# Slots of the preparation in the shared scans: statistics three slots earlier, one more slot between engines, projected halves loaded four slots apart

## The chip, the core and the metric

The kernel runs on one core of a Trainium2 chip. The metric is the device time of one execution in microseconds, taken as the median of several runs. Below, PE is TensorE's matmul stream and PEld its weight loads, DVE is VectorE, ACT is ScalarE, POOL is GpSimd, and SP is the queue of SyncE, which here issues most of the DMAs. A line number such as L571 is a line of the kernel before.

## The reference

The input x has 32 sequences of 256 tokens with 256 channels. A recurrent block comes first, then two layers of windowed attention with a gated feed-forward, all in float32:

```python
xr, gate = split(x @ W_in.T, 2);  xr = xr + t_emb[:, None]      # 512 channels each
xc = silu(causal depthwise conv of 4 taps over time (xr) + b_conv)
xn = layernorm(xc) * ln_g + ln_b
Bm, Cm, dt = split(xn @ W_xproj.T, 3)                           # 16 states each
Ad = 1 + tanh(dt @ W_dt.T + b_dt) * 0.01 * A
Bd = Bm * minimum(norm(xn), 1.0)
h  = clip(h * Ad + outer(Bd, xn), -10, 10);  y_t = C_t . h      # one step per token
cond = ((y + D * xn) * silu(gate)) @ W_out.T
for l in range(2):  # attention: 8 heads of 64, rotary, window 128; FFN: 682 gated, GELU
    c = c + attention(shift(c)) @ wo;   c = c + ffn(shift(c))
out = x + c
```

The step over tokens is serial: 256 steps per sequence, each on the whole state.

## The kernel before

**Groups and chunks.** The 32 sequences are four groups of eight (`GB`). One scan serves a whole group: 16 states by 8 sequences fill the 128 partitions, and the 512 channels lie along the row, so a step is one instruction on VectorE, `step` (L716), on a tile of 128x512. The 256 tokens are cut into eight chunks of 32 steps (`CH`), so there are 32 chunks in all; a chunk's 256 rows (8 sequences by 32 tokens) are handled in two halves of 128 (`NJ`).

**Who runs beside whom.** Group 0's scan runs by itself (`alone` in the code). The scans of groups 1 to 3 share the chip with attention and feed-forward of the group before. The last group's attention runs when all scans are over. `scan_slots` merges the agendas of all scans into one list of slots, one slot for each step, and the main loop emits some slots after each of the eight stages that a sequence takes in a layer.

**The agenda.** `at(s, f, ...)` puts the call of f at slot s; `s0 = c * CH` is the slot of a chunk's first step, and its preparation has negative offsets, inside the steps of the chunk before. Two agendas are filled: the first mostly with work of VectorE, ScalarE and GpSimd, the second mostly with work of TensorE and SP. Within one slot the first comes ahead of the second. The slots are not yet the order on the chip: the program's order serves as priority, and a scheduler reorders each engine's instructions by readiness and priority. Only what is wrapped in `tc.keep_in_program_order` (the shift L571, the figures L609 and the scaling of rows L706) keeps its order among itself.

**What prepares a chunk**, in the order of the data:

1. For groups 1 to 3, the input half of the projection was computed during group 0's scan and written to DRAM. `load_projected` (L447, SP) loads it back in two pieces xp of two channel blocks each. They share two buffers with xg, the input that `load_x` (L455) loads for the gate's `project` (L399, TensorE, ps_in).
2. `conv_in` adds the condition (L472, DVE) and takes the first tap (L478, POOL); `conv_taps` takes the other three (L489, DVE); `conv_th` (L504, ACT) and `conv_out` (L509, DVE) make silu of it in xc. There are four blocks of channels, two slots apart. xr and acc have two buffers each, xc has one.
3. `raw_sums` (L518, TensorE, ps_raw) multiplies xc by the state weights; `raw_copy` (L526, ACT) and `raw_turn` (L533, three DMAs issued by ACT) bring it to the scan's partitions as rw.
4. For each half j: `norm_turn` (L548, TensorE) transposes xc into the PSUM tile tp_x. `norm_stats` (L558, DVE) takes mean and variance from it and POOL raises the variance to the power of minus one half (L565). `norm_shift` (L571, DVE) makes the bias. `norm_apply` (L579, ACT) writes xn from tp_x, which frees the bank. `norm_affine` (L586, L587, POOL) applies gain and bias. `norm_out` stores xn to DRAM as xnd (L591, SP) and sums its squares (L593, ACT, sq_x).
5. `length` (L599 DVE, L600 POOL) and `figures` (L609, DVE) turn the statistics into rhs; `figures_out` (L618, TensorE, ps_st) spreads it; `figures_in` (L630 to L636, DVE) joins it with rw; `decay_th` (L643, ACT) and `decays` (L648 to L661, DVE and POOL) give beta, ct and the limits. `put_c` (L669, POOL) fills the read-out weights ly.

**What follows a step.** `load_rows` (L685, SP) fetches a token's eight rows of xnd, each spread over 16 partitions, into xrep (six buffers); `scale_row` (L706, ACT) multiplies them by beta; the step (L716) consumes them; `read_out` (L728, TensorE, y) sums over the states. `load_skip`, `skip` (L758, POOL, xd), `gated`, `out_turn` (tz) and `out_gate` (L799, DVE, zT) complete a chunk, `project_y` (L808, ps_out), `copy_y` (L819, ACT, yo) and `put_y` store it for `load_res` (L956, SP), with which attention begins.

**The other side.** Names of attention and feed-forward that appear below: ps_qkv (L989) the projection of q, k and v; sq, ss, swp, rot and rn (L1002 to L1022) the norms and the rotary on DVE and POOL; tr_qk (L1028) their transposition, and qT, kT (L1033) its copy by ACT; v_sb (L1172); sc (L1191, L1198) the scores and pT (L1207) their exponentials; rs and ov (L1228, L1247) sums and values; rinv and rb (L1236, L1259) the inverse sums, sent through DRAM; oT (L1254) the division; ps_wo (L1039); ve and rstd (L1301, L1303), hT (L1329) the layer norm; pa (L1351), ag (L1362 ACT, L1369 DVE) the wide part of the feed-forward; po_f (L1378) and fo (L1389) its narrow part.

**PSUM.** All matmul outputs take their banks from one pool:

```python
ps_w = ctx.enter_context(tc.tile_pool(name="psw", bufs=8, space=PSUM, reuse_waits="tile"))
```

It has eight banks and one tag, so tp_x, ps_raw, ps_st, ps_in and y of the scan compete for them with all outputs of attention and feed-forward.

Of the kernel before, what the change touches and what calls it, by code (L numbers as in the profile page):

```python
# [73 lines left out]
def kernel(  # L74
# [88 lines left out]
    for j in range(NJ):  # L163
# [18 lines left out]
        out=mask_t[:, 0:W], in_=mask_t[:, 0:W], compare_op=ALU.is_ge, fill=MASKED_LOW,  # L182
# [3 lines left out]
        out=mask_t[:, W : 2 * W], in_=mask_t[:, W : 2 * W], compare_op=ALU.is_ge,  # L186
# [35 lines left out]
    def program(ctx, exact):  # L222
# [154 lines left out]
        def group_scan(g):  # L377
# [8 lines left out]
            alone = g == 0  # L386
# [5 lines left out]
            def at(s, what, *args):  # L392
                agendas[-1].setdefault(s, []).append(partial(what, *args))
# [285 lines left out]
            def by_tensor(t):  # L679
                return alone and t % (2 * NQ) < XR  # L680
# [172 lines left out]
            for c in range(NCH):  # L853
                for t in range(CH):
                    at(c * CH + t, step, c, t)
            for c in range(NCH):
                s0 = c * CH
                for hb in range(CH // TB):
                    s = s0 + hb * TB
                    for i in range(NI):  # L860
                        at(s + 4 * i + 5, read_out, c, hb, i)
                    at(s + 21, gated, c, hb)
                    at(s + 25, out_gate, c, hb)
                    at(s + 11, skip, c, hb)
                for ch in range(NC_):
                    at(s0 - 38 + 2 * ch, conv_in, c, ch)
                    at(s0 - 37 + 2 * ch, conv_taps, c, ch)
                    at(s0 - 36 + 2 * ch, conv_th, c, ch)
                    if not alone:
                        at(s0 - 35 + 2 * ch, conv_out, c, ch)  # L870
                for ch, s in enumerate((13, 16, 17, 18)):
                    at(s0 + s + 2, gate_th, c, ch)
                    if not alone:
                        at(s0 + s + 4, gate_out, c, ch)
                at(s0 - 25, raw_copy, c)
                at(s0 - 24, raw_turn, c)
                for j in range(NJ):
                    s = s0 - 26 + 4 * j
                    at(s + 2, norm_stats, c, j)
                    at(s + 4, norm_shift, c, j)  # L880
                    at(s + 5, norm_apply, c, j)
                    at(s + 6, norm_affine, c, j)
                    at(s + 9, norm_out, c, j)
                at(s0 - 11, length, c)
                at(s0 - 9, figures, c)
                at(s0 - 7, figures_in, c)
                at(s0 - 6, decay_th, c)
                at(s0 - 5, decays, c)
                at(s0 - 4, put_c, c, 0)
                at(s0 + 4, put_c, c, 1)  # L890
                for d in range(KM):
                    at(s0 + 45 + 2 * d, copy_y, c, d)
                    at(s0 + 46 + 2 * d, put_y, c, d)
            agendas.append({})
            for c in range(NCH):
                s0 = c * CH
                at(s0 - 43 if alone else s0 + 6, load_x, c)
                if alone:
                    for ch in range(NC_):
                        at(s0 - 40 + 2 * ch, project, c, ch)  # L900
                else:
                    for i in range(2):
                        at(s0 - 44 + 2 * i, load_projected, c, i)
                for ch, s in enumerate((13, 16, 17, 18)):
                    at(s0 + s, project, c, NC_ + ch)
                at(s0 - 27, raw_sums, c)
                for j in range(NJ):
                    at(s0 - 26 + 4 * j, norm_turn, c, j)
                at(s0 - 8, figures_out, c)
                for t in range(CH):  # L910
                    if not by_tensor(t):
                        at(s0 + t - 6, load_rows, c, t)
                    if by_tensor(t) and t % XR == 0:
                        at(s0 + t - 4, spread_rows, c, t)
                    at(s0 + t - 2, scale_row, c, t)
                for hb in range(CH // TB):
                    s = s0 + hb * TB
                    at(s - 9 if alone else s + 7, load_skip, c, hb)
                    at(s + 23, out_turn, c)
                for d in range(KM):  # L920
                    at(s0 + 43 + 2 * d, project_y, c, d)

            if alone:
                n = (NG - 1) * NCH * 2
                for u in range(n):
                    s = -30 + u * (NCH * CH) // n
# [6 lines left out]
        def scan_slots(groups):  # L933


            slots, scans = {}, [group_scan(g) for g in groups]
            for part in range(2):
                for i, agendas in enumerate(scans):
                    for s, what in agendas[part].items():
                        slots.setdefault(i * S + s, []).extend(what)  # L940
            for s in range(min(slots), max(slots) + 1):
                for what in slots.get(s, ()):
                    what()
                yield s
# [104 lines left out]
        if exact:  # L1049
# [4 lines left out]
                out=mask[:, 0:W], in_=mask[:, 0:W], compare_op=ALU.is_ge, fill=MASKED,  # L1054
# [3 lines left out]
                out=mask[:, W : 2 * W], in_=mask[:, W : 2 * W], compare_op=ALU.is_ge, fill=MASKED,  # L1058
# [448 lines left out]
        s0 = done[0]  # L1507
# [130 lines left out]
```

## Time and profile before

| | |
|---|---|
| Median of 3 runs | 3618.64 us (3616.05 to 3620.17) |
| Profiled execution, its own time | 3624.1 us |
| Its span (first to last instruction) | 3622.3 us |
| TensorE busy | 3510.2 us, 97% |
| VectorE busy | 2666.1 us, 74% |
| ScalarE busy | 2151.6 us, 59% |
| GpSimd busy | 1801.9 us, 50% |
| Steps (L716) | 1024, 954.0 us, 932 ns each |
| First step of group 0, first of group 1, last of group 3 | 57, 447.8 and about 2828 us after the span's start |
| Period of a chunk from chunk 18 on | 102.85 us |

How to read it: the span counts from the first to the last instruction of the profiled execution, and its own time is 1.8 us longer. A share is busy time over the span. An engine's busy time says only how long it executed instructions. In a group's row, "idle before" is the engine's idle time just ahead of these instructions with what ended it, and in a row of a wait the three numbers are the total, the count and the longest in us. TensorE's ends are modelled, so its busy share says little about how close to its peak it works.

### The profile page before, as it was taken

What the parts mean: (1) busy time and instruction counts of PE and PEld (TensorE: products, weight loads), DVE (VectorE), ACT (ScalarE), POOL (GpSimd) and SP (SyncE); (2) the same over time, 40 slices, a digit from 0 to 9 for tenths busy, and PEclk for the clock granted to TensorE, in tenths of its full rate; (3) what the DMA queues carried; (4) which work ended last, traced back from release to release, by engine and by line L of the source; (5) the groups of instructions that cost most, each with busy time, mean ns of one, the idle gap of its engine ahead of it and who ended that gap; (6) DMA issues with size and microseconds to landing.
All of it is one profiled execution on the core that took longest, in us unless ns stands there. A gap on an engine that the chain in (4) does not pass through costs nothing.

```text
span 3622.3 us, 56212 instructions
## 1 busy us (share of the span) xinstructions
PE 3510.2 (97%) x19548; PEld 2282.4 (63%) x19548; DVE 2666.1 (74%) x5049; ACT 2151.6 (59%) x3659; POOL 1801.9 (50%) x1746
## 2 busy tenths in 40 slices
PE   8999989999999999999999999999999999999999
PEld 5445335666666666666666666666666677777677
DVE  5888889888787877887787778877777545555553
ACT  3666656666666666666666666666666444544443
POOL 4333456545455555645455556455544454544551
PEclk8999989999999999999999999999999999999999
DMA  7888755445454645444454554544454112011111
GB/s 192 212 218 217 197 155 149 133 111 137 129 141 123 154 137 151 123 113 128 118 139 125 137 150 135 137 107 130 115 138 120 54 45 62 13 30 36 34 27 37
DMA packets 468763, 435.59 MB, mean 120 GB/s; under 512 B 228724, under 2 KB 308085, under 8 KB 468341
## 3 DMA queue, kind: packets, MB, share of 16 engines
q1 hardware_dynamic: 384018, 419.88, 42.9%
q10 hardware_dynamic: 84450, 12.01, 2.0%
q8 instruction: 158, 2.59, 0.3%
q14 instruction: 137, 1.11, 0.1%
HBM read 383.54 MB, written 46.66 MB: 119 GB/s over the span
## 4 chain that ended last, share of the span: by engine, by line
PE 63%; DVE 16%; DMA 7%; POOL 6%; ACT 4%; issue 3%; SPq 1%; ACTq 0%; DVEq 0%; POOLq 0%
PE ps_qkv L989 13%; PE pa L1351 13%; PE po_f L1378 7%; DVE h L716 6%; DMA xrep<-xnd 5%; PE ps_wo L1039 4%; PE y L728 4%; PE sc L1198 4%; PE ov L1247 3%; PE ps_out L808 3%; PE tr_qk L1028 2%; DVE acc L489 2%; ACT xrep L706 2%; PE rs L1228 2%; PE ps_in L399 2%
## 5 line engine op out<-in xcount | busy, mean ns | idle before, releaser
L716 DVE CUSTOM_DVE_ANT_0 h<-h,xrep,lim 128x512 f32<-128x512 f32 x1024 | 954.0, 932 | 233.7 <-ACT xrep L706 198.4
L706 ACT ACTIVATE xrep<-xrep,beta 128x512 f32<-128x512 f32 x960 | 674.0, 717 | 367.4 <-DMA xrep<-xnd 280.8
L989 PE MATMUL ps_qkv<-qkv,res 128*128 128x512 f32 x1536 | 718.6, 603 | 22.2 <-DVE ag L1369 9.9
L1351 PE MATMUL pa<-hT,w 128*128 128x256 f32 (+1 forms) x2816 | 680.1, 383 | 1.2 <-ACT oT L1254 0.4
L1351 PEld LDWEIGHTS pa<-hT,w 128*128 128x128 f32 (+1 forms) x2816 | 515.3, 188 | 147.1 <-issue 57.1
L1013 POOL TENSOR_TENSOR rot<-rot,swp 128x512 f32<-128x512 f32 x256 | 335.7, 1311 | 444.7 <-DVE swp L1010 339.0
L989 PEld LDWEIGHTS ps_qkv<-qkv,res 128*128 128x128 f32 x1536 | 281.7, 191 | 314.2 <-issue 241.8
L1021 POOL TENSOR_TENSOR rn<-ss,neg_half 128x8 f32<-128x8 f32 x256 | 459.5, 1795 | 17.9 <-DVE ss L1019 7.9
L728 PE MATMUL y<-h,ly 128*32 128x512 f32 x2048 | 346.5, 611 | 12.5 <-DVE h L716 11.4
L1303 POOL TENSOR_TENSOR rstd<-ve,neg_half 128x2 f32<-128x2 f32 x64 | 46.3, 723 | 608.2 <-DVE ve L1301 605.0
L1378 PE MATMUL po_f<-ag,w 128*128 128x256 f32 x1280 | 307.9, 388 | 4.9 <-DVE fo L1389 4.9
L1022 POOL TENSOR_TENSOR rot<-rot,rn 128x512 f32<-128x512 f32 x256 | 291.8, 1140 | 20.1
L1369 DVE SCALAR_TENSOR_TENSOR ag<-pa,b_sb,ag 128x256 f32<-128x256 f32 x320 | 152.6, 477 | 198.8 <-ACT ag L1362 198.6
L1378 PEld LDWEIGHTS po_f<-ag,w 128*128 128x128 f32 x1280 | 236.5, 191 | 69.2 <-issue 12.8
L1002 ACT ACTIVATE sq<-ps_qkv 128x512 f32<-128x512 f32 x256 | 151.7, 596 | 210.1 <-PE ps_qkv L989 148.9
L1362 ACT ACTIVATE ag<-pa,b_sb 128x256 f32<-128x256 f32 x320 | 150.1, 469 | 176.3 <-PE pa L1351 173.9
L489 DVE SCALAR_TENSOR_TENSOR acc<-xr,wc_sb,acc 128x256 f32<-128x256 f32 x384 | 193.4, 528 | 57.6 <-POOL acc L478 57.1
L1039 PE MATMUL ps_wo<-oT,wo 128*128 128x256 f32 x1024 | 231.7, 379 | 0.7 <-ACT ag L1362 0.7
L1005 DVE TENSOR_TENSOR rot<-ps_qkv,rc_sb 128x512 f32<-128x512 f32 x256 | 175.1, 684 | 77.0 <-ACT sq L1002 76.7
L1198 PE MATMUL sc<-qT,kT 64*128 64x128 f32 (+1 forms) x2048 | 220.5, 344 | 0.0
L1207 ACT ACTIVATE pT<-sc 128x512 f32<-128x512 f32 x384 | 208.5, 596 | 12.2 <-PE sc L1198 10.2
L1198 PEld LDWEIGHTS sc<-qT,kT 64*128 64x128 f32 x2048 | 150.8, 187 | 99.8 <-issue 92.7
(159 smaller groups left out, 5656.2 us busy)
## 6 DMA issues: line engine op xcount, KB each, us to landing
xrep<-xnd SPq DMA_DIRECT2D x960, 256.0 KB
rb<-inv SPq DMA_DIRECT2D x128, 256.0 KB
xnd<-xn SPq DMA_DIRECT2D x64, 256.0 KB
qkv<-in_wqkv_dram SPq DMA_DIRECT2D x24, 512.0 KB
ahead<-xs_a SPq DMA_DIRECT2D x48, 256.0 KB
xp<-ahead SPq DMA_DIRECT2D x48, 256.0 KB
xd<-xnd SPq DMA_DIRECT2D x192, 64.0 KB
w<-in_w_dram SPq DMA_DIRECT2D x80, 128.0 KB
```

The source lines that it names most:

```text
L489: nc.vector.scalar_tensor_tensor(acc, xr[:, :, k : k + CH], wc_sb[:, ch, k : k + 1], acc, ALU.mult, ALU.add,)
L706: scaled = nc.scalar.activation(bx, ck[c].pop(("bx", t), bx), AF.Copy, scale=ck[c]["beta"][:, t : t + 1])
L716: nc.vector._custom_dve(TENSOR_ADD_SAT, out=h_new, in0=state["h"], in1=bx, s0=ck[c]["lim"][:, 0, t : t + 1], s1=ck[c]["lim"][:, 1, t : t + 1],
L728: nc.tensor.matmul(ck[c]["y", hb][32 * q : 32 * q + 32, :], ly[hb % 2][:, 32 * t : 32 * t + 32], ck[c].pop(("h", hb * TB + t)), start=(i = ...
L989: nc.tensor.matmul(ps, res[b][:, k, t0 : t0 + W], wt["qkv", a][:, k], start=(k == 0), stop=(k == KM - 1),)
L1013: nc.gpsimd.tensor_add(rot, rot, swp)
L1021: nc.gpsimd.tensor_tensor(rn, ss, neg_half, ALU.pow)
L1022: nc.gpsimd.tensor_mul(rot, rot, bc(rn, 2, DH))
L1039: nc.tensor.matmul(po[:, d], wt["wo", 0][:, c, d * P : (d + 1) * P], oT[:, c, :], start=(c == 0), stop=(c == NC_ - 1),)
L1198: nc.tensor.matmul(banks[r][:, i, :], kT[rows, i0 + i, kw * W : (kw + 1) * W], qT[rows, i0 + i, kw * W :], start=self.apart, stop=self.apa ...
L1351: nc.tensor.matmul(dst[x], wt["w1", m][:, k, x], self.h[:, k], start=(k == 0), stop=(k == KM - 1),)
L1378: nc.tensor.matmul(self.po[:, d], wt["w2", 0][:, m, d * P : (d + 1) * P], self.ag[m], start=(m == 0), stop=(m == len(MCH) - 1),)
```

## The change

For the scans of groups 1 to 3 (not `alone`), the calls of a chunk's preparation get other slots. No instruction is added, removed or resized.

- Convolution, raw sums with copy and turn, the transposes `norm_turn` and `norm_stats` move three slots ahead (`early = 3`).
- `norm_shift` moves two slots ahead, `norm_apply` and `norm_affine` one; `norm_out` stays. Between statistics and shift there are then three slots instead of two, between shift and apply two instead of one; between `norm_affine` and `norm_out` there are four instead of three.
- `length`, `figures`, `figures_out` and `figures_in` move one slot ahead. `decay_th`, `decays`, `put_c` and all that follows a step stay.
- The first half of the projection is still loaded at slot s0 - 44, the second at s0 - 40 instead of s0 - 42.
- Group 0's scan keeps its slots.

```diff
@@ -853,6 +853,7 @@
             for c in range(NCH):
                 for t in range(CH):
                     at(c * CH + t, step, c, t)
+            early = 0 if alone else 3
             for c in range(NCH):
                 s0 = c * CH
                 for hb in range(CH // TB):
@@ -863,27 +864,32 @@
                     at(s + 25, out_gate, c, hb)
                     at(s + 11, skip, c, hb)
                 for ch in range(NC_):
-                    at(s0 - 38 + 2 * ch, conv_in, c, ch)
-                    at(s0 - 37 + 2 * ch, conv_taps, c, ch)
-                    at(s0 - 36 + 2 * ch, conv_th, c, ch)
+                    at(s0 - early - 38 + 2 * ch, conv_in, c, ch)
+                    at(s0 - early - 37 + 2 * ch, conv_taps, c, ch)
+                    at(s0 - early - 36 + 2 * ch, conv_th, c, ch)
                     if not alone:
-                        at(s0 - 35 + 2 * ch, conv_out, c, ch)
+                        at(s0 - early - 35 + 2 * ch, conv_out, c, ch)
                 for ch, s in enumerate((13, 16, 17, 18)):
                     at(s0 + s + 2, gate_th, c, ch)
                     if not alone:
                         at(s0 + s + 4, gate_out, c, ch)
-                at(s0 - 25, raw_copy, c)
-                at(s0 - 24, raw_turn, c)
+                at(s0 - early - 25, raw_copy, c)
+                at(s0 - early - 24, raw_turn, c)
                 for j in range(NJ):
                     s = s0 - 26 + 4 * j
-                    at(s + 2, norm_stats, c, j)
-                    at(s + 4, norm_shift, c, j)
-                    at(s + 5, norm_apply, c, j)
-                    at(s + 6, norm_affine, c, j)
-                    at(s + 9, norm_out, c, j)
-                at(s0 - 11, length, c)
-                at(s0 - 9, figures, c)
-                at(s0 - 7, figures_in, c)
+                    if alone:
+                        shift, apply, affine, out = 4, 5, 6, 9
+                    else:
+                        shift, apply, affine, out = 2, 4, 5, 9
+                    at(s - early + 2, norm_stats, c, j)
+                    at(s + shift, norm_shift, c, j)
+                    at(s + apply, norm_apply, c, j)
+                    at(s + affine, norm_affine, c, j)
+                    at(s + out, norm_out, c, j)
+                e = 0 if alone else 1
+                at(s0 - e - 11, length, c)
+                at(s0 - e - 9, figures, c)
+                at(s0 - e - 7, figures_in, c)
                 at(s0 - 6, decay_th, c)
                 at(s0 - 5, decays, c)
                 at(s0 - 4, put_c, c, 0)
@@ -900,13 +906,13 @@
                         at(s0 - 40 + 2 * ch, project, c, ch)
                 else:
                     for i in range(2):
-                        at(s0 - 44 + 2 * i, load_projected, c, i)
+                        at(s0 - 44 + 4 * i, load_projected, c, i)
                 for ch, s in enumerate((13, 16, 17, 18)):
                     at(s0 + s, project, c, NC_ + ch)
-                at(s0 - 27, raw_sums, c)
+                at(s0 - early - 27, raw_sums, c)
                 for j in range(NJ):
-                    at(s0 - 26 + 4 * j, norm_turn, c, j)
-                at(s0 - 8, figures_out, c)
+                    at(s0 - early - 26 + 4 * j, norm_turn, c, j)
+                at(s0 - (8 if alone else 9), figures_out, c)
                 for t in range(CH):
                     if not by_tensor(t):
                         at(s0 + t - 6, load_rows, c, t)
```

## The prediction, made before the changed kernel was run

> **What bounds the kernel now.** I read the busy row of the page first, then busy time by stretch, then the waits of TensorE in the stretch where later groups' scans run beside attention, then single instructions. The busy row says which engine can set the time:
>
> ```profile
> PE 3510.2 (97%) x19548; PEld 2282.4 (63%) x19548; DVE 2666.1 (74%) x5049; ACT 2151.6 (59%) x3659; POOL 1801.9 (50%) x1746
> PE 63%; DVE 16%; DMA 7%; POOL 6%; ACT 4%; issue 3%; SPq 1%; ACTq 0%; DVEq 0%; POOLq 0%
> ```
>
> TensorE is busy for 97% of the 3622.3 us span; the chain that ended last lies on it for 63%, and the 16% on VectorE are mostly the first scan, which runs alone. The stretches show where TensorE is not full (columns: window, length, busy time of PE, PEld, DVE, ACT, POOL, then clock, DMA share, GB/s):
>
> ```profile
> 300.00:600.00 300.00, 272.15 (x1169) 124.31 (x1162) 262.37 (x474) 181.59 (x327) 149.95 (x168) 0.95 0.69 181
> 600.00:900.00 300.00, 292.65 (x1697) 191.95 (x1693) 255.70 (x475) 196.31 (x337) 164.58 (x157) 0.99 0.47 126
> 900.00:1200.00 300.00, 288.70 (x1649) 187.64 (x1646) 240.76 (x460) 193.19 (x332) 156.41 (x152) 0.99 0.52 132
> 1500.00:1800.00 300.00, 296.96 (x1745) 196.04 (x1746) 240.49 (x466) 194.59 (x332) 158.73 (x149) 1.00 0.45 121
> 2700.00:3000.00 300.00, 300.00 (x1752) 206.28 (x1749) 170.18 (x324) 160.98 (x258) 132.93 (x108) 1.00 0.27 77
> ```
>
> Once the last scan is over (after about 2830 us) TensorE is full, so nothing that the change touches shortens that tail. Before it, what can be gained is TensorE's idle time. Its waits from 620 to 2760 us (total us, times, longest us) are small and nearly all on VectorE or ScalarE releasing a PSUM bank:
>
> ```profile
> PE sc L1191 <- DVE ag L1369: 10.5, 10, 1.5
> PE ps_qkv L989 <- DVE ag L1369: 9.9, 12, 1.2
> PE ps_qkv L989 <- DVE rinv L1236: 4.5, 8, 0.9
> PE po_f L1378 <- DVE fo L1389: 4.4, 2, 3.1
> ```
>
> With a dozen smaller rows they come to 43 us in 2140 us. That is the ceiling of any gain there. The waits that the change is aimed at are on other engines:
>
> ```profile
> ACT xrep L706 <- DMA xrep<-xnd: 158.0, 66, 5.6
> ACT xn L579 <- DVE stat L571: 97.2, 27, 7.1
> POOL xn L586 <- ACT xn L579: 73.2, 36, 7.4
> ```
>
> ScalarE's 97.2 us for the normalization's statistic is real, but ScalarE is only 65% busy (194.6 of 300 us in the stretch from 1500), and TensorE does not stop during it. One instance, with the work in order of time:
>
> ```profile
> 1533.48 1.71 POOL L758 TENSOR_TENSOR xd<-xd,dskip_sb 128x512 f32<-128x512 f32 x1
> 1535.15 0.55 POOL L565 TENSOR_TENSOR stat<-ve,neg_half 128x1 f32<-128x1 f32 x1
> 1535.73 0.16 DVE L571 SCALAR_TENSOR_TENSOR stat<-mv,stat 128x1 f32<-128x1 f32 x1 [1.66 <-POOL stat L565]
> 1535.92 0.78 ACT L579 ACTIVATE xn<-tp_x,stat 128x512 f32<-128x512 f32 x1 [5.05 <-DVE stat L571]
> ```
>
> ScalarE stands 5.05 us because the 0.55 us power on GpSimd (L565) is queued behind the rotary work and xd.
>
> [...] L565 above sits behind xd though its input was ready. So what counts is the order on each engine, which the scheduler makes anew from the slots. [...] Accordingly I count TensorE by starts: dense matmuls with 512 columns follow each other 430 ns apart here.
>
> **The change, part by part.** No instruction is added or removed; all 56212 stay, and every duration too. In a scan that shares the chip a slot (one step) takes 102.85/32 = 3.2 us and a chunk of 32 steps 102.85 us. Groups 1 to 3 have 24 chunks, of which 14 (18 to 31) repeat the same pattern.
>
> *Convolution, three slots earlier.* In the realized order VectorE's conv work (L472, L489, L509) does not move in the repeating chunks: buffers for xr, xc and xp hold it, and it is already some 240 us ahead of its chunk's first step, the last xc some 137 us. Cost 0, either way at most the 1.3 us sc waits that conv work ahead of ag on VectorE causes (10.5 us in all).
>
> *Halves of the projection (xp, L447) at slots −44 and −40 instead of −44 and −42,* while conv_in goes three earlier: load to use shrinks from six and eight slots to three and three, about 10 us. SP's order in the repeating chunks barely shifts; a load takes some us, and VectorE waited for xp five times, 4.3 us in all. I take 0; bounds 0 to +5. [...] (SPq L447 waited 82.6 us for ps_in, longest 10.0). The second load three slots nearer its buffer's release waits less, which could also give back a few us.
>
> *Raw sums, transposes, statistics, shift, apply, affine.* In the order of the new kernel statistics come about three steps earlier, shift and length two, figures one, xnd's stores (two DMAs a chunk on SP) two. POOL's order stays: L565 is still behind the rotations and xd. So the ScalarE stall shrinks only by the extra slot, and covers nothing on TensorE: 0. The xnd stores stood 63 and 76 us ahead of their chunk's first step, so earlier is worth nothing to the scan. The transposed tile tp_x is written earlier by more than xn frees it: its PSUM bank is held some 10 us instead of 7, twice a chunk. That is a cost on the scarce resource: 0 to 0.5 us a chunk.
>
> *Scaling of rows (L706) at the chunk's boundary.* With figures a slot earlier the scheduler puts row scalings in order. Before, a scaling ahead of its turn waited for its rows, and VectorE for it:
>
> ```profile
> 1599.43 0.72 ACT L706 ACTIVATE xrep<-xrep,beta 128x512 f32<-128x512 f32 x1 [3.50 <-DMA xrep<-xnd]
> 1601.28 0.81 DVE L716 CUSTOM_DVE_ANT_0 h<-h,xrep,lim 128x512 f32<-128x512 f32 x1 [3.64 <-ACT xrep L706]
> 1602.98 0.48 DVE L1369 SCALAR_TENSOR_TENSOR ag<-pa,b_sb,ag 128x256 f32<-128x256 f32 x1
> 1603.52 1.55 PE L989 MATMUL ps_qkv<-qkv,res 128*128 128x512 f32 x3 [0.86 <-DVE ag L1369]
> ```
>
> That late ag cost TensorE 0.86 us, and 0.22 us behind rinv at 1597.69: 1.1 us × 14 = 15 us to gain. Against it, the copies qT and kT (L1033), which free the bank that the next pa wants, now queue behind four scalings (2 × 0.72 us more than before) and a wait for beta, 2.41 us before: I estimate 1 us × 14 = 14 us lost (0 to 1.5 us, over up to 24 chunks). The raw copy and its issues (1.89 us of ScalarE's queue) now precede the exponentials of the first scores; they have 2 to 4 us of slack, 0. Net −1 us, between −15 and +30.
>
> *Start of group 1 (400 to 620 us).* TensorE waited 4.62 us at 480.27 for the first residual load, whose issue now stands seven xrep loads earlier on SP. But VectorE is 90% busy there, and the work ahead of attention's first division on it is the same (395 us in both orders). I keep half, rounded: −5 us (−10 to +4).
>
> *Irregular chunks (620 to 1500 us).* TensorE's starts there lose about 8.5 us per 100 us against dense streaming, 5.5 in the repeating part, 4.6 with no scan at all. The difference of 3 is 26 us; a reordering may shift that either way, I take −4 (−20 to +15).
>
> Sum: 0 + 0 − 1 − 5 − 4 = −10 us. The profiled execution took 3624.1 us (3622.3 of span and 1.8 around it), 5.5 above the median 3618.64: 3614.1 there, **3608.6** as a median.
>
> **Rivals.** *No change:* the preparation had 60 us of slack, TensorE has the same work, and the waits removed are off its path. For it: the 5.05 us ScalarE stall with no TensorE gap. Time 3612 to 3626. *Slower by bank pressure:* qT, kT and tp_x hold banks longer. It decides when the tr_qk bank comes free later than pa wants it (1594.2 in the chunk above); at 1.5 us × 24 = 36 less the 15 gained, 3640. For it: eight banks, and every large TensorE wait is a bank. Against: the removed stall is measured, the delay only worked out from the order. *Larger gain:* most of the 43 us of waits and the start vanish together, 3585. Against: the waits have several releasers, of which one is addressed. *Not doing what it says:* conv does not move at all in the repeating part; that is inside my forecast.
>
> **How the numbers follow.** A measurement here tells about 0.2%, 7.2 us, from no change. My case (a few us to 25 us gained) 0.46, the larger gain 0.11, no change 0.18, slower by banks or by a late xp load 0.25. From these: faster by over 0.2% 0.57, within 0.2% 0.18, slower 0.25. The range 3588 to 3634 leaves out most of the larger gain and the end of the slower case. The likeliest case's own range is 3593 to 3611.
>
> **What would show it.** Right: busy time of TensorE the same, ps_qkv waiting for ag less than 9.9 us, the scaling's 3.50 us stall gone from the chunk's boundary, xn still waiting for stat, little gained after 1500 us. Wrong: pa or tr_qk waiting for qT/kT or xn (banks), VectorE waiting for xp, SP waiting at L447, a scan that ends later than 2827 us, or a shorter tail after it.

## The result, and the profile after

The changed kernel is slower: 3629.39 us (median of 8 runs, 3626.1 to 3634.6) against 3618.67 us (median of 8, 3613.61 to 3622.52), a ratio of 1.0033 with an interval of 1.0023 to 1.0043, or 12 us by the ratio (the medians lie 10.7 us apart). Forecast were 3608.6 us and a gain of 10. The time lies inside the range that was given, on the other side.

Lines from 916 on stand six lower in the changed kernel: ag is L1368 and L1375, sc L1197, ps_qkv L995. First the page's busy row and chain of the changed kernel:

```profile
PE 3509.3 (97%) x19548; PEld 2277.7 (63%) x19548; DVE 2646.2 (73%) x5049; ACT 2151.2 (59%) x3659; POOL 1824.2 (50%) x1746
PE 68%; DVE 16%; DMA 5%; POOL 4%; issue 3%; ACT 3%; SPq 0%; ACTq 0%; DVEq 0%; POOLq 0%
```

No engine's busy time has grown by more than 23 us, and TensorE's is the same (3509.3 us after 3510.2; a second profile of before, experiment 9, has 3495.1). So the loss is not one of more work; order, waits and the clock remain. TensorE's waits of the whole run, changed kernel (total us, times, longest), the row that grew and two small ones:

```profile
PE sc L1197 <- DVE ag L1375: 29.8, 15, 2.7
...
PE ov L1253 <- DVE ag L1375: 3.8, 9, 2.0
...
PE pa L1357 <- ACT qT L1039: 0.6, 1, 0.6
```

Before, the scores waited 10.5 us for ag, ps_qkv 9.9 for ag and 4.5 for rinv. The two rows of ps_qkv are gone, as forecast; the row of sc has grown by 19.3 us. All of TensorE's waits from 620 to 2760 us together rose only from 43.3 to 47.4 us, so they are not the whole loss. Waiting for qT, which I had feared at 14 us, is 0.6. On ScalarE and VectorE the waits that the change was aimed at did shrink (changed kernel, whole run):

```profile
ACT xrep L706 <- DMA xrep<-xnd: 247.2, 154, 5.9
ACT xn L579 <- DVE stat L571: 96.8, 44, 4.6
DVE h L716 <- ACT xrep L706: 81.4, 67, 3.5
```

VectorE's steps wait 81.4 us for scaled rows instead of 198.4. That bought nothing by itself: the kernel is slower all the same.

**Where the new wait sits.** It comes once in each chunk from 16 to 28, at the stage that runs beside rows 23 to 26 of a chunk. One place, changed kernel, timeline of ScalarE, VectorE and TensorE in order of time (start, duration, engine, line, work; in brackets the idle time before it and what ended it):

```profile
2087.71 1.33 ACT L706 ACTIVATE xrep<-xrep,beta 128x512 f32<-128x512 f32 x2
2094.86 0.72 ACT L706 ACTIVATE xrep<-xrep,beta 128x512 f32<-128x512 f32 x1 [5.81 <-DMA xrep<-xnd]
2095.59 1.28 ACT L1368 ACT_TABLE_LOAD   x1
2096.89 0.47 ACT L1368 ACTIVATE ag<-pa,b_sb 128x256 f32<-128x256 f32 x1
2097.40 0.48 DVE L1375 SCALAR_TENSOR_TENSOR ag<-pa,b_sb,ag 128x256 f32<-128x256 f32 x1 [1.07 <-ACT ag L1368]
2097.93 0.38 PE L1197 MATMUL sc<-mask_t,ident_b 128*128 128x512 bf16 x1 [2.66 <-DVE ag L1375]
```

ScalarE scales two rows, and then stands 5.81 us on a third whose row has not landed. Behind it in the queue are the 1.28 us table load and the feed-forward's ag. VectorE's ag waits for that, and it is ag that frees the bank which the scores want: TensorE stands 2.66 us. The same place in the kernel before:

```profile
2087.15 1.28 ACT L1362 ACT_TABLE_LOAD   x1
2088.45 0.47 ACT L1362 ACTIVATE ag<-pa,b_sb 128x256 f32<-128x256 f32 x1
2094.69 0.47 DVE L1369 SCALAR_TENSOR_TENSOR ag<-pa,b_sb,ag 128x256 f32<-128x256 f32 x1
2095.12 0.72 ACT L706 ACTIVATE xrep<-xrep,beta 128x512 f32<-128x512 f32 x1 [5.09 <-DMA xrep<-xnd]
2095.21 0.38 PE L1191 MATMUL sc<-mask_t,ident_b 128*128 128x512 bf16 x1 [1.34 <-DVE ag L1369]
```

There a row out of turn waits too, 5.09 us (another one, R798 in the order below), but ScalarE's ag has gone ahead of it. TensorE stands only 1.34 us, for VectorE's ag, which comes at 2094.69 behind other work of VectorE. The order on ScalarE in the two built kernels, chunk 24, shows the exchange. Rows are numbered through all four scans (R797 is row 29 of the chunk), v is v_sb, TABLE a table load, and the dots leave out some entries:

```
before: v R791 R792 TABLE ag sq R798 sq R793 R794 ag ... ag R800 qT kT R797 R802 ag oT R804 oT R799
after:  v R791 R792 R797 TABLE ag sq R798 sq R793 R794 ag ... ag R799 R800 R801 R802 qT kT ag oT oT
```

So the changed order is better at the chunk's boundary (right half) and worse at the place before it. The rows are scaled out of turn in both kernels. My description of the kernel was wrong in this: with `keep_in_program_order` around every scaling of these scans, R798 still stands ahead of R793 in both. Row 797 cannot be early: with six xrep buffers its load needs step 791 to be over. That step took from 2090.00 to 2090.81, the load was issued at 2090.84 and the scaling began at 2094.86.

**What follows a wait of this length.** In some chunks TensorE's granted clock is halved just after it, here to 0.51. Windows of the changed kernel after the wait above (window, length, busy time of PE, PEld, DVE, ACT, POOL, clock, DMA share, GB/s):

```profile
2098.50:2101.90 3.40, 3.40 (x16) 0.97 (x14) 3.39 (x9) 3.37 (x6) 2.41 (x2) 0.51 0.95 312
2101.90:2106.00 4.10, 4.10 (x23) 3.60 (x20) 4.10 (x12) 3.72 (x6) 4.02 (x4) 1.00 0.43 121
```

The clock records of the changed kernel have seven such stretches of 3.4 us between 1300 and 2500 us. Half of that time is my estimate of what they cost, about 12 us. In windows of 300 us from 1500 to 2700 us the clock is 0.99 throughout in this kernel. In experiment 1, the other one with a row ahead of ag at this place, it is 0.99 up to 2100 us and 1.00 after that. In the kernel before and in experiments 2 to 7, 9 and 12 it is 1.00 in all four. With the 4 us by which the waits grew this makes 16 us, against 12 measured (chunks 8 to 17 became somewhat shorter). So by this estimate the larger part of the loss is not the longer wait but the slow clock after it. The period of a chunk, from the starts of the steps (mean of chunks 18 to 30), went from 102.84 us to 103.82. Over 13 chunks that is 13 us, the size of the whole loss.

### The profile page after: what moved, and what is told of

It reads as the page before. It is cut to its first block, busy times and chain, and to the rows that moved or that the text cites. A ratio compares the mean times of both kernels' runs of the same rounds, so it can differ in the third digit from the quotient of the medians.

```text
span 3627.1 us, 56166 instructions
## 1 busy us (share of the span) xinstructions
PE 3509.3 (97%) x19548; PEld 2277.7 (63%) x19548; DVE 2646.2 (73%) x5049; ACT 2151.2 (59%) x3659; POOL 1824.2 (50%) x1746
## 4 chain that ended last, share of the span: by engine, by line
PE 68%; DVE 16%; DMA 5%; POOL 4%; issue 3%; ACT 3%; SPq 0%; ACTq 0%; DVEq 0%; POOLq 0%
PE pa L1357 14%; PE ps_qkv L995 14%; PE po_f L1384 7%; DVE h L716 6%; PE y L728 5%; PE ps_wo L1045 5%; PE ov L1253 4%; PE sc L1204 4%; DMA xrep<-xnd 4%; PE ps_out L808 3%; PE tr_qk L1034 3%; PE ps_in L399 2%; PE rs L1234 2%; DVE acc L489 2%; POOL acc L478 2%
## 5 line engine op out<-in xcount | busy, mean ns | idle before, releaser
L716 DVE CUSTOM_DVE_ANT_0 h<-h,xrep,lim 128x512 f32<-128x512 f32 x1024 | 948.2, 926 | 138.8 <-ACT xrep L706 81.4
L995 PE MATMUL ps_qkv<-qkv,res 128*128 128x512 f32 x1536 | 712.7, 600 | 2.4 <-ACT oT L1260 2.4
L995 PEld LDWEIGHTS ps_qkv<-qkv,res 128*128 128x128 f32 x1536 | 282.0, 191 | 283.9 <-issue 251.9
L1027 POOL TENSOR_TENSOR rn<-ss,neg_half 128x8 f32<-128x8 f32 x256 | 444.2, 1735 | 28.3 <-DVE ss L1025 16.8
L728 PE MATMUL y<-h,ly 128*32 128x512 f32 x2048 | 356.2, 620 | 13.9 <-DVE h L716 12.4
L1309 POOL TENSOR_TENSOR rstd<-ve,neg_half 128x2 f32<-128x2 f32 x64 | 55.2, 863 | 586.6 <-DVE ve L1307 569.1
L1375 DVE SCALAR_TENSOR_TENSOR ag<-pa,b_sb,ag 128x256 f32<-128x256 f32 x320 | 151.7, 474 | 226.8 <-ACT ag L1368 226.8
L1028 POOL TENSOR_TENSOR rot<-rot,rn 128x512 f32<-128x512 f32 x256 | 305.0, 1191 | 18.8
L1368 ACT ACTIVATE ag<-pa,b_sb 128x256 f32<-128x256 f32 x320 | 151.5, 473 | 204.3 <-PE pa L1357 200.3
L1045 PEld LDWEIGHTS ps_wo<-oT,wo 128*128 128x128 f32 x1024 | 195.6, 191 | 27.7 <-PE sc L1204 0.8
```

The costliest lines, as they stand in the source:

```text
L716: nc.vector._custom_dve(TENSOR_ADD_SAT, out=h_new, in0=state["h"], in1=bx, s0=ck[c]["lim"][:, 0, t : t + 1], s1=ck[c]["lim"][:, 1, t : t + 1],
L728: nc.tensor.matmul(ck[c]["y", hb][32 * q : 32 * q + 32, :], ly[hb % 2][:, 32 * t : 32 * t + 32], ck[c].pop(("h", hb * TB + t)), start=(i = ...
L995: nc.tensor.matmul(ps, res[b][:, k, t0 : t0 + W], wt["qkv", a][:, k], start=(k == 0), stop=(k == KM - 1),)
L1027: nc.gpsimd.tensor_tensor(rn, ss, neg_half, ALU.pow)
L1028: nc.gpsimd.tensor_mul(rot, rot, bc(rn, 2, DH))
L1045: nc.tensor.matmul(po[:, d], wt["wo", 0][:, c, d * P : (d + 1) * P], oT[:, c, :], start=(c == 0), stop=(c == NC_ - 1),)
```

## The experiments

Theory O: the loss is ScalarE's order at this place. Rivals: B, PSUM banks held longer by transposes that moved ahead; X, xp loaded too late for the convolution. All ratios are to the kernel before, run beside each on the same chip. Its median was 3619.4 us beside experiments 1 to 4, 3622.3 beside 5 to 8 and 3615.45 beside 9 to 12, so ratios are to be compared, not times.

**1. The convolution alone.**

```diff
+            early = 0 if alone else 3
-                    at(s0 - 38 + 2 * ch, conv_in, c, ch)
+                    at(s0 - early - 38 + 2 * ch, conv_in, c, ch)
                     (conv_taps, conv_th and conv_out alike)
```

> The kernel before, with conv_in, conv_taps, conv_th and conv_out of groups 1 to 3 three slots earlier and nothing else. Theory O (ScalarE's order): the loss comes from one place in each chunk from 17 to 29, where a third row scaling, that of the chunk's row 29, is put ahead of the feed-forward's ag on ScalarE and waits there some 5.8 us for its row; the order of this kernel has it there too, so the wait of sc for ag should be 20 to 30 us as in the changed kernel (before: 10.5), and the time 3624 to 3632. Theory B (banks: tp_x and ps_raw are held longer because statistics and transposes moved): these did not move here, so 3616 to 3621 and a wait of about 10 us.

3629.91 us, ratio 1.0037 (1.0023 to 1.0051). TensorE's waits:

```profile
PE sc L1197 <- DVE ag L1375: 25.0, 13, 2.5
...
PE pa L1357 <- ACT qT L1039: 6.3, 7, 1.2
```

This is what theory O expected. A loss of the same size comes with the convolution's four slots alone, though its own instructions do not move on VectorE in the repeating chunks. A wait appears beside it that the changed kernel hardly has: pa for the bank of qT, 6.3 us, which is the wait that the prediction's slow rival named. The period is 103.83 us, and four half-clock stretches of 3.4 us lie after 1300 us.

**2. Figures and xp alone.** The changed kernel with `early = 0` and shift, apply, affine at 4, 5, 6.

> The changed kernel without its three slots ahead and without the extra slots between engines: only length, figures and their matmul one slot earlier and the second half of the projection loaded at slot -40. Theory O: the order of the row scalings at the place named is that of the kernel before, so 3615 to 3622 and a wait of sc for ag of about 10 us. Theory X (the later load of xp makes VectorE's convolution late, which delays the release of ag's bank): 3624 to 3632, with VectorE waiting for xp.

3612.03 us, ratio 0.9975 (0.9964 to 0.9985), period 102.14 us: better than either theory had it. The wait of sc for ag is 12.6 us, and VectorE waits for xp 2.9 us in all, so theory X is out. Part of the change helps. Experiments 10 and 11 take the two apart.

**3 and 4. Rows scaled in order,** in the changed kernel and in the kernel before:

```diff
                     tc.keep_in_program_order(scaled)
+                    if state.get("sc"):
+                        tc.add_manual_dep(
+                            scaled.ins, state["sc"],
+                            mybir.DependencyInfo(
+                                mybir.DependencyClass.NoSync, mybir.DependencyReason.DATA
+                            ),
+                            reason="rows in order",
+                        )
+                    state["sc"] = scaled.ins.name
```

> The changed kernel, with each row scaling of groups 1 to 3 kept behind that of the row before it on ScalarE (an ordering edge, no wait). Theory O: row 29 no longer stands ahead of ag, the wait of sc for ag falls from 29.8 us to under 12, ScalarE's 5.8 us waits for a row beside ag go, and the time falls by 8 to 20 us against the changed kernel, to 3609 to 3621. Theory B: banks are held as before, 3626 to 3632.

3591.81 us, ratio 0.9921 (0.9908 to 0.9935), period 101.66 us. The wait of sc for ag falls to 13.4 us, not quite to the 12 expected, and the gain is larger than expected: 1.1% faster than the changed kernel by the two ratios.

> The kernel before with the same ordering edge between row scalings. Theory O: the stall at the chunk's boundary (3.5 us on ScalarE, 0.86 us of ps_qkv behind ag) goes, since it too came from a scaling ahead of its turn: the wait of ps_qkv for ag falls from 9.9 us to under 3, the time to 3603 to 3614. If the order of scalings has little to do with TensorE's waits: 3615 to 3622.

3584.58 us, ratio 0.9900 (0.9885 to 0.9915), period 101.50 us: the lowest ratio of all kernels run here, though experiments 7 and 8 are within its interval, and again a larger gain than expected. Lines below the edit stand eight lower, so ag is L1370 and L1377, and the step L724. Waits of TensorE (whole run) and of ScalarE (620 to 2780 us) in this kernel:

```profile
PE sc L1199 <- DVE ag L1377: 10.6, 10, 1.5
```

```profile
ACT xrep L706 <- DMA xrep<-xnd: 15.0, 13, 2.5
ACT xrep L706 <- DVE beta L654: 6.0, 3, 2.7
```

The scalings' wait for rows falls from 158.0 us to 15.0 in this part of the run, and ps_qkv no longer appears in TensorE's list as waiting for ag. TensorE's waits from 620 to 2760 us fall from 43.3 to 20.4 us. So a scaling out of turn costs TensorE far less than its own wait, and it does so through what stands behind it. Some 12 us of the 35 gained lie outside TensorE's waits and are not traced.

**5. Transposes, statistics, shift, apply, affine alone,** with the convolution at its old slots.

```diff
-                    at(s + 2, norm_stats, c, j)
+                    at(s - early + 2, norm_stats, c, j)
-                    at(s0 - 26 + 4 * j, norm_turn, c, j)
+                    at(s0 - early - 26 + 4 * j, norm_turn, c, j)
-                        shift, apply, affine, out = 4, 5, 6, 9
+                        shift, apply, affine, out = 2, 4, 5, 9
```

> The kernel before, with the transposes and statistics three slots earlier and shift, apply and affine moved with the extra slots between engines; convolution, raw sums, figures and xp at their old slots. Theory O: the order of the row scalings beside ag stays that of the kernel before, so 3615 to 3623. Theory B (tp_x holds its banks longer): 1 us in each of 24 chunks, about 3640, with new waits of TensorE for xn or st.

3631.47 us, ratio 1.0026 (1.0017 to 1.0034), period 103.34 us. Theory O has no loss here, and theory B named the wrong wait but the right resource. A row is new among TensorE's waits:

```profile
PE ps_qkv L995 <- DVE ag L1375: 9.5, 12, 0.9
PE ps_qkv L995 <- DVE xd L779: 6.3, 13, 0.5
```

and one instance of it in the timeline of TensorE:

```profile
2128.19 0.66 PE L548 MATMUL tp_x<-ident,xc 128*128 128x128 f32 x4
...
2133.84 1.55 PE L995 MATMUL ps_qkv<-qkv,res 128*128 128x512 f32 x3 [0.47 <-DVE xd L779]
```

At the same place of the kernel before, the transposed tile comes behind ps_qkv:

```profile
2129.08 1.98 PE L989 MATMUL ps_qkv<-qkv,res 128*128 128x512 f32 x4
...
2133.86 0.66 PE L548 MATMUL tp_x<-ident,xc 128*128 128x128 f32 x4
```

The transposed tile now takes a bank 5.6 us ahead of this ps_qkv. So, most likely, ps_qkv has to wait for the bank of y, which xd frees: 0.5 us in each repeating chunk, which agrees with the period. That is 6.3 of some 9 us; the rest is not traced. In the changed kernel this wait does not appear, so losses of single parts do not add.

**6. One scaling of 32 in order.** The changed kernel, with the edge of experiment 3 for `t == 29` only.

> The changed kernel with an ordering edge for one row of 32 only: the scaling of row 29 of each chunk stays behind the scaling emitted before it. Theory O, in its narrow form: this one scaling ahead of ag is the whole loss, so the wait of sc for ag falls from 29.8 us to 10 to 14 and the time by 10 to 18 us against the changed kernel, to 3611 to 3620. If the loss of the changed kernel is spread over all scalings out of order: 3624 to 3630, with the wait still over 20 us.

3602.09 us, ratio 0.9946 (0.9932 to 0.996), period 101.68 us. The place looks like this (line numbers eight higher again than in the changed kernel):

```profile
2068.89 1.33 ACT L706 ACTIVATE xrep<-xrep,beta 128x512 f32<-128x512 f32 x2
2070.24 1.28 ACT L1376 ACT_TABLE_LOAD   x1
2071.53 0.47 ACT L1376 ACTIVATE ag<-pa,b_sb 128x256 f32<-128x256 f32 x1
2077.95 0.38 PE L1205 MATMUL sc<-mask_t,ident_b 128*128 128x512 bf16 x1 [1.50 <-DVE ag L1383]
```

ag stands ahead of the late row again, and the wait of sc for ag is 12.9 us. This edge, one per chunk, turned +0.33% into -0.54%: 0.87% by the ratios, or some 31 us, twice what I expected. Per repeating chunk it is 103.82 less 101.68, 2.1 us. TensorE's gaps of over 0.25 us between 1500 and 2780 us fall from 23.9 to 8.7 us in total, 1.2 us a chunk, and the five half-clock stretches of that part, by the same estimate 0.7 us a chunk, are gone (clock 1.00 in all windows from 1500 to 2700 us).

The edge moves more than one scaling, though. It lets the chunk's boundary run in order a row further (R797 to R802), and R798, which stood ahead of the second sq, goes with R797. At this place R798 hardly mattered: the second sq starts 10.39 us after the two scalings here (2079.28), and 10.76 us after them in the kernel before, with R798 ahead of it. What the boundary adds is not separated.

**7. Figures, xp and rows in order,** in the kernel before.

> The kernel before with all row scalings in order, and with figures a slot earlier and the second xp load at slot -40. If the 7 us that these two gave came from an earlier beta at the chunk's boundary, a wait of its own, they add to the 34.8 us of the ordering edge: 3574 to 3581. If the edge has already taken the same stall away: 3582 to 3588.

3587.25 us, ratio 0.9902 (0.9887 to 0.9917). No more than the edge alone, as the second expectation had it. Most likely the edge has taken the same stall: in experiment 4 the scalings already wait only 6.0 us for beta. A small gain of its own is not ruled out by the intervals.

**8. Group 1 at its old slots,** otherwise as experiment 3 (`early = 0 if g < 2 else 3`, and so on).

> The changed kernel with all row scalings in order, but with group 1's slots as before, so that only groups 2 and 3 have the change. The changed kernel with rows in order was 7.2 us slower than the kernel before with rows in order, and the two traces differ by that much by 700 us, when attention has just begun. If the change costs at this start: 3582 to 3588. If it costs in every chunk: 3588 to 3592.

3588.08 us, ratio 0.9904 (0.9889 to 0.9919), at the edge of both expectations. Against experiment 3 (0.9921) it is 6 us less, but the intervals overlap. Its 97th matmul into ps_qkv starts at 636.6 us and that of experiment 3 at 646.4; with the scatter of the start that experiment 9 shows, one profile of each does not settle it. That the change costs at the start of attention is likely, not shown.

**9. The kernel before once more.**

> The kernel before once more, for a second profile, since the first profiled execution was 5.5 us above the median. If the chunk period of the repeating part is 102.8 us again and the start is shorter, the first profile's excess lies in the start; if the period differs, chunk periods of single profiles cannot be compared to 0.2 us.

One run of 3609.38 us. The chunk period is 102.78 us, so the period repeats within 0.1 us in these two profiles. The 97th matmul into ps_qkv starts at 627.3 us instead of 640.0: nearly all of the difference between the two profiles (3607.5 and 3622.3 us of span) lies in the start. Up to 640 us the clock was at half for 75 us in the first profile and for 41 us in this one (mean clock of the whole span 0.988 and 0.994); half of the difference, an estimate of what it costs, is 17 us.

**10 and 11. Figures alone, xp alone.**

```diff
-                at(s0 - 11, length, c)
+                at(s0 - e - 11, length, c)
                 (figures, figures_out and figures_in alike)
```

```diff
-                        at(s0 - 44 + 2 * i, load_projected, c, i)
+                        at(s0 - 44 + 4 * i, load_projected, c, i)
```

> The kernel before with length, figures, figures_out and figures_in one slot earlier, nothing else. If the gain of 7 us that figures and xp gave together is beta's (the wait of row scalings for beta fell from 39.7 to 10.4 us): 3610 to 3616 where the kernel before has 3619 to 3622. If xp gave it: 3617 to 3623.

> The kernel before with the second half of the projection loaded at slot -40, nothing else. The counterpart: 3617 to 3623 if figures gave the gain, 3610 to 3616 if this did; above 3626 if the shorter time from load to use costs.

Figures: 3611.14 us, ratio 0.9985 (0.9977 to 0.9994). xp: 3617.57 us, ratio 1.0002 (0.9991 to 1.0014). Waits of the row scalings for beta in 620 to 2780 us, figures first, then xp:

```profile
ACT xrep L706 <- DVE beta L654: 10.2, 3, 4.2
```

```profile
ACT xrep L706 <- DVE beta L654: 39.7, 17, 2.9
```

The gain, some 5 us, is that of figures, most likely by an earlier beta, whose wait fell from 39.7 us. The later xp load costs nothing that is clear of noise, as forecast.

**12. The convolution alone, with row 29 in order.**

> The kernel before with the convolution alone three slots earlier, and the ordering edge for row 29's scaling. Theory O: the convolution's move both puts the rows at the chunk's boundary in order (a gain) and row 29 ahead of ag (a loss of 2.1 us in each of 13 chunks); without the loss 3595 to 3606, as with all of the change and the edge (3602). If the gain at the boundary needs figures and statistics moved: 3614 to 3622.

3597.3 us, ratio 0.9949 (0.9932 to 0.9967), as theory O expected and as with all of the change (0.9946). One slot move thus does both: it straightens the rows at the boundary, and it puts row 29 ahead of ag. Why the scheduler answers to the convolution's slots in this way was not traced; the built order and the runs show that it does.

## Why the prediction was wrong

- **What bounds the kernel:** right. TensorE's busy time is unchanged, the tail has the same length, and 117 us less of VectorE's waits for rows did not pay. The 43 us of waits as a ceiling were not: experiment 4 gained 35 us while these waits fell by 23, so part of the gain lay outside TensorE's idle time. The longest of these waits, 4.1 us of po_f for ag_rem, was for data and not for a bank. The 5.05 us stall of ScalarE was read rightly: in the kernel before, the input of L565 (ve, L562) was written from 1529.03 to 1529.18, GpSimd worked without a gap until xd ended at 1535.19, and L565 began at 1535.15.
- **The convolution, costed at 0: the step that failed.** I checked where its own instructions stand on VectorE, found them unmoved, and stopped. Their slots are priorities, and the scheduler answered on another engine. I had looked at one chunk boundary and not at the stage ahead of it, where the same comparison of orders shows R797 ahead of ag. In its place the runs show 0.37% lost by this part alone, and 31 us regained by an edge on one scaling a chunk. The sum also had no term for the clock, and half-clock stretches cost about 12 us by my estimate. The bound of 1.3 us on the sc waits was the wait of before, carried over to an order that no longer held.
- **The scaling of rows at the boundary, -1:** the mechanism was right (both waits of ps_qkv went, 14.4 us in all against 15 expected), the cause named was not: the convolution moves it, not figures. The price set against it, 14 us for qT and kT, was nearly nothing: 0.6 us, though three more scalings stand ahead of qT in the built order and not two. In experiment 1 it was 6.3 us.
- **Figures:** costed inside the boundary only; measured at -0.15%, most likely since beta is ready earlier.
- **Statistics, 0 with an end of 0.5 us a chunk:** in the kernel before, the end was the truth (experiment 5); in the changed kernel the wait does not show.
- **xp, 0:** right. The few us that a shorter wait of the second load could give back were an estimate, and experiment 11 does not show them (ratio 1.0002). **Irregular chunks, -4:** the sign fits (mean period of chunks 8 to 17 is 93.61 us after 94.60 and 94.06). **Start, -5:** the first ps_qkv came 8.2 us earlier than in the first profile of before, and by the 97th it was 2.4 us late; against the second profile of before it was 1.3 and 15.1 us late. The sign is not that of my -5, but the start scatters by 12.7 us between two profiles of one kernel, so its size stays open.
- **The rival on the slow side** had the right resource, a bank that comes free late, at the wrong place. It priced tr_qk at 1594.2; the bank was that of pa, held by ag, behind a row. One sign of being wrong that I had named came true: the last step of the scans starts at 2832.2 us, after 2827.2. That the time still fell within my range was luck: its slow end stood for held banks and a late xp, not for what happened.

## What to carry to other kernels

Where a scheduler sets the order, moving one stage's slots can leave that stage where it was and swap two instructions of others; compare the whole period on every engine, not the moved lines. Look first for instructions that wait for a transfer, and ask what stands behind each: here one row scaling that stood ahead of ag once in 32 steps, and on which ScalarE stood 5.81 us in the chunk shown, decided between 0.3% slower and 0.5% faster. Keeping such instructions in the order in which their data arrive was worth 1.0%, more than any of the slot moves.

## What the hardware showed beside this

Between 1300 and 2530 us, TensorE waits of 2.00 to 2.75 us were followed by 3.4 us at half clock seven times in the changed kernel (clock 0.51 to 0.53 in windows of 3.4 to 3.6 us), and waits of 2.06 to 2.34 us four times in experiment 1. Others of the same length were not: in the changed kernel those of 2.00 us up to 1577.07, 2.01 us up to 1994.03 and 2.42 us up to 2515.75 (clock 1.00 in the 13 to 16 us after each), and one of 2.52 us at 2305.23 in experiment 1. Neither were the shorter ones: 1.69 and 1.96 us in the changed kernel, and up to 1.49 us in the kernel before, whose clock is 1.00 from 1300 to 2700 us. Around the seven waits TensorE had 1.25 to 2.00 us of matmuls in 4 us (1.34 around the one shown above), and around the one at 2515.75, which was not followed, 1.58. So neither the length of a wait nor the work around it decides alone here, and what does is open.
